# A transformer block on one core: smaller pieces in the gaps between attention scores, rows turned through DRAM

## The chip, the core and the metric

One core of a Trainium2 chip runs the whole program. Its engines work side by side, each through its own list in order: TensorE (PE; its weight loads are shown as PEld), VectorE (DVE), ScalarE (ACT), GpSimd (POOL), and SyncE (SP), which here issues nearly all DMAs. The metric is the device time of one launch in microseconds. Everything is fp32.

## The reference

A pre-norm block: attention with grouped heads and a rotary embedding, then a gated feed-forward part. x is 4 x 512 x 512 (batch, time T, width D), with 32 query heads of 16, 8 key heads, and F = 1376. Cut to what matters:

```python
def attn(x, Wq, Wk, Wv, Wo):
    q, k, v = heads(x @ Wq), heads(x @ Wk), heads(x @ Wv)
    q = q * cos + rotate_half(q) * sin
    k = k * cos + rotate_half(k) * sin
    att = einsum("bhgqd,bhkd->bhgqk", q, k) / sqrt(16)
    att = where(causal, att, -inf)
    ctx = einsum("bhgqk,bhkd->bhgqd", softmax(att), v)
    return merged(ctx) @ Wo

def ffn(x, W_gate, W_up, W_down):
    return (silu(x @ W_gate.T) * (x @ W_up.T)) @ W_down.T

x = x + attn(layernorm(x), Wq, Wk, Wv, Wo)
x = x + ffn(layernorm(x), W_gate, W_up, W_down)
```

## The kernel before

The order of all instructions on every engine is the order in which the Python code issues them; buffers, banks and semaphores follow from it. A matrix product in the code appears in the trace as two passes of TensorE, each with its weight load.

**Groups and visits.** The 4 batches have 8 groups of 4 heads each, 32 in all (`GROUPS`: batch, a pair of two groups `m`, which half `hf`). While group g is exponentiated and averaged, the plain scores of group h = g + 2 are computed to find the greatest of each row, which is then written into rows of `qa` so that the scores of the second computation come out less that value. `slot(b, steps)` does the eight groups of a batch. Each group has four *visits*: `both_scores` (plain scores, L477, in the pair of banks `plain`; the transposed scores less the greatest, L482, in the pair `less`), `exponentials` on ACT (L550), `all_greatest` on DVE (L500, two heads of 512, or of 384 and 128, columns), then `odd_steps(us)`, DVE work from queues, and `gap()`, TensorE work from the slot's list. Then comes `last_visit` (both pairs of banks are used for scores of 256 columns), `turned_round(h)` (a small DVE transpose, L537, and its DMA; `laid_out` reads it back into `qa`), and `averages(g)`: 16 products into the one bank `av` (L576). With `hf == 1` a pair `m` is complete: `later` gets the reads of `av` into `cx` and `us` (L590, L594), a shuffle (L598), four reciprocals (L602), each pair of them with a POOL product into `cx` (L605). `averages` begins with `while unread: do(later)`, since `av` must be read before it is written again; until then `later` is taken from its front.

**The slot's list.** `gap()` takes from the list as much as 1/32 of its total cost says (`fill`; costs are in microseconds). In the first slot it is what is left of batch 1's projections, then those of batches 2 and 3, each behind four `turned` steps; all three batches are attended in later slots. In slots two to four it is the output projection of the batch before (`attended`, L376), its feed-forward part (`hidden`, L420) and the down projection (`down`, L445). `projections` makes keys, queries in four parts, and values of a batch; `portions` cuts a product into steps. A product's bank is one of three (`bank()`, pool `ps_mm`). What follows a product (`finish`: for keys and queries `rotated`, two DVE and two POOL or DVE instructions, L266 to L269) runs at once where `thin[0]` is false; in the opening and the first slot it is put into `full`, with a cost of 1.42.

**The queues of DVE work.** `odd_steps` takes, until its time is down to 0.4, from `full`, from `aside` (statistics of a tile of rows, then its normalisation and, with it, its transpose), from `later`. At the end of `slot` and where a step is due, the queue is emptied by force: `turned`'s `tail(i)` takes from `aside` until tile i is there.

**Turning rows.** Products need the rows' transpose (`xnT`). Batches 0 and 1 are transposed by TensorE against an identity (`transposed`, L221, copy by ACT or DVE, L226 and L224). For the others, and for the rows of every `attended`, `flipped` does it: a DVE transpose of 32 x 32 blocks (L231, two buffers), four DMAs to DRAM (L235), and, for the tile before (at the last tile for both), a read of 256 KB into `xnT` (L237). SP issues these in order, between the weights (L159) and the rows of the greatest (L538, L547).

**The opening.** Rows of batch 0 are normalised, transposed and projected (keys, first query, values), then two masked queries are made on POOL (`masked`, L465), then the plain scores and minima of groups 0 and 1 run with the other queries of batch 0, the transposes of batch 1 and its keys and first query between them. POOL's `rstd` power (L185) is part of the statistics.

Of the kernel before, what the change touches and what calls it, by code (L numbers as in the profile page):

```python
# [15 lines left out]
ALU = mybir.AluOpType  # L16
# [3 lines left out]
NH, NKV, DH = 32, 8, 16  # L20
FF = 1376
P = 128
NT = T // P
NK = D // P
# [50 lines left out]
def preln_block_kernel(  # L75
# [13 lines left out]
    nc = tc.nc  # L89
# [72 lines left out]
    full = deque()  # L162
    thin = [True]

    def bank():
        while len(full) > 1:
            full.popleft()[1]()
        return ps_mm.tile([P, T], F32, tag="mm", name="mm")


# [27 lines left out]
    def do(queue, n=1):  # L198
        for _ in range(min(n, len(queue))):
            queue.popleft()[1]()  # L200

    def odd_steps(us, banks=True):

        for n in range(len(soon)):
            left, step = soon.popleft()
            if left > 0:
                soon.append((left - 1, step))
            else:
                aside.appendleft(step)
        while us > 0.4:  # L210
            others = (unread and later) or aside or later
            queue = (full or others) if banks else (others or full)
            if not queue:
                return
            us -= queue[0][0]
            do(queue)

    def transposed(xn, i, xnT):
        pt = bank()
# [5 lines left out]
        else:  # L225
            nc.scalar.copy(xnT[:, :, ts(i, P)], src)  # L226

    def flipped(xn, i, n, dst):

        t = work.tile([P, D], F32, tag="g", name="xt", bufs=2)  # L230
        nc.vector.transpose(t, xn)  # L231
        turned = flip[n].rearrange("(c d) (i r s) -> i r d c s", d=32, r=4, s=32)
        for r in range(4):
            rows = t[32 * r : 32 * r + 32, :]
            nc.sync.dma_start(out=turned[i, r], in_=rows.rearrange("d (c s) -> d c s", s=32))  # L235
        for a in [i - 1, i] if i == NT - 1 else [i - 1] if i > 0 else []:
            nc.sync.dma_start(out=dst[:, :, ts(a, P)], in_=flip[n].rearrange("(k p) t -> p k t", p=P)[:, :, ts(a, P)])  # L237

    def portions(products, finish, n=2, us=0.0):

        made = {}

        def part(a):
            if a == 0:
                made["ps"] = bank()
            for step in products[len(products) * a // n : len(products) * (a + 1) // n]:
                step(made["ps"])
            if a == n - 1:
                if thin[0]:
                    full.append((us, lambda: finish(made["ps"])))  # L250
                else:
                    finish(made["ps"])

        return [lambda a=a: part(a) for a in range(n)]

    def projected(w, m, xnT, finish):
        def product(ps, k):
            nc.tensor.matmul(ps, lhsT=w[:, k, ts(m, P)], rhs=xnT[:, k, :], start=k == 0, stop=k == NK - 1)  # L258

        steps = [lambda ps, k=k: product(ps, k) for k in range(NK)]  # L260
        return [(0.86, step) for step in portions(steps, finish, 4, 1.42)]

    def rotated(ps, dst, engine=nc.gpsimd):

        rot = work.tile([P, T], F32, tag="rot", name="rot", bufs=4)
        nc.vector.stream_shuffle(rot, ps, ROTATE)  # L266
        engine.tensor_tensor(rot, rot, sin, ALU.mult)
        nc.vector.tensor_tensor(dst, ps, cos, ALU.mult)
        engine.tensor_tensor(dst, dst, rot, ALU.add)  # L269

    def both_steps(measure, norm, tiles=range(NT), cost=1.2):

        for i in tiles:
            yield 1.05, lambda i=i: measure(i)
            if i > 0:
                yield cost, lambda i=i: norm(i - 1)
            if i == NT - 1:
                yield cost, lambda i=i: norm(i)

    def projections(b, n, early=False):  # L280

        home, xa, found, xn = homes[n], {}, {}, {}
        xnT = xnT_of[b]

        def load(i):
# [9 lines left out]
        def norm(i):  # L295
            xn[i] = work.tile([P, D], F32, tag="xa", name="xa", bufs=4) if early else xa[i]
            normalised(xn[i], found[i])
            if b > 1:
                flipped(xn[i], i, b % 2, xnT)

        def keys():
            def finish(ps):
                kr = work.tile([P, T], F32, tag="rot", name="kr", bufs=4)
                rotated(ps, kr, nc.vector if early else nc.gpsimd)

                def spread():
                    ks = work.tile([P, T], F32, tag="rot", name="ks", bufs=4)
                    nc.vector.stream_shuffle(ks, kr, SWAP)
                    for t, hf, src in ((0, 0, kr), (1, 1, kr), (0, 1, ks), (1, 0, ks)):
                        nc.gpsimd.tensor_scalar(  # L310
                            home[:, 4 + 2 * t + hf, :], src, halves[hf], (one16, one0)[hf], ALU.mult, ALU.add
                        )

                if early:
                    spread()
                else:
                    soon.append((1, (0.75, spread)))

            return projected(wk_sb, 0, xnT, finish)

        def vals():
            def product(ps, i, k):
                nc.tensor.matmul(
                    ps[:, ts(i, P)],
                    lhsT=xnT[:, k, ts(i, P)],
                    rhs=wv_sb[:, k, :],
                    start=k == 0,
                    stop=k == NK - 1,
                )

            def finish(ps):
                nc.scalar.copy(
                    values(n)[:, :, :, DH : 2 * DH].rearrange("p i g d -> p (i g) d"),
                    ps.rearrange("p (a d) -> p a d", d=DH),
                )

            steps = [lambda ps, i=i, k=k: product(ps, i, k) for i in range(NT) for k in range(NK)]
            return [(0.9, step) for step in portions(steps, finish, 4)]

        def queries(m):  # L340
            engine = nc.vector if early and m == 0 else nc.gpsimd
# [2 lines left out]
        def begin():  # L344
            for i in range(NT):
                load(i)
            aside.extend(both_steps(measure, norm, cost=1.2 if b > 1 else 0.6))

        def tail(i):
            while i not in xn:  # L350
                do(aside)
            if b < 2:
                transposed(xn[i], i, xnT)

        turned = [(0.45 if b < 2 else 0.0, lambda i=i: tail(i)) for i in range(NT)]
        rest = [*keys(), *queries(0), *vals()]
        for m in range(1, 4):
            rest += queries(m)
        return (0.0, begin), turned, rest

    def attended(b):

        found, xn = {}, {}

        def measure(i):
            found[i] = statistics(xr[b, i])
# [1 line left out]
        def norm(i):  # L368
            xn[i] = work.tile([P, D], F32, tag="xa", name="xn", bufs=4)
            normalised(xn[i], found[i])  # L370
            flipped(xn[i], i, b % 2, xnTs[0])

        def outp(i):
            def product(ps, m):
# [1 line left out]
                nc.tensor.matmul(ps, lhsT=cx[m][:, ts(i, P)], rhs=wo_sb[:, m, :], start=m == 0, stop=m == 3)  # L376

            def finish(ps):
                nc.vector.tensor_tensor(xr[b, i], ps, xr[b, i], ALU.add)
                aside.extend(both_steps(measure, norm, [i]))  # L380

            return [(1.72, step) for step in portions([lambda ps, m=m: product(ps, m) for m in range(4)], finish)]

        def tail():
            while NT - 1 not in xn:
                do(aside)

        def begin():
            if (b, 0) not in xr:
# [1 line left out]
                    load_xr(b, i)  # L391

        first = [(0.0, begin), *(step for i in range(NT) for step in outp(i))]
        return first, [(0.0, tail)]

    wgu = {}

# [11 lines left out]
    def hidden(b, n):  # L409
# [3 lines left out]
        def half(f, a):  # L413
# [8 lines left out]
                )  # L422

            def finish(ps):
                if a == 0:
                    gs[f] = work.tile([P, T], F32, tag="g", name="g", bufs=2)

# [191 lines left out]

    for i in range(NT):  # L620
        load_xr(0, i)
    load_w(wk_sb, wk)
    nc.sync.dma_start(out=rope_sb, in_=rope)
    load_columns(wq_sb, wq, 0, P)
# [8 lines left out]
    load_w(wv_sb, wv)  # L633
    load_columns(wq_sb, wq, P, D)
    load_w(wo_sb, wo)
    for t in low:
        nc.gpsimd.memset(t, 0.0)
    nc.gpsimd.memset(values(0), 1.0)
    thin[0] = False
    for cost, step in turned:  # L640
        step()
    for cost, step in start[:2]:
        step()
    do(aside, len(aside))
    for cost, step in start[2:8]:
        step()
    masked(0)
    masked(1)
    for n in range(1, 4):
        nc.gpsimd.memset(values(n), 1.0)  # L650
    for cost, step in start[8:12]:
        step()


# [15 lines left out]
        return done  # L670

    thin[0] = True
    opening = deque([*start[12:], *turned1, *rest1[:8]])
    each = sum(cost for cost, _ in opening) / 6
    done = 0.0
    for h in range(2):
# [17 lines left out]
    def slot(b, steps):  # L694
# [12 lines left out]
        for g in groups:  # L707
# [6 lines left out]
            for n, visit in enumerate(visits):  # L714
# [13 lines left out]
                all_greatest(h, visit)  # L728
                if n == 2:
                    do(later_act)  # L730
                odd_steps((1.9, 1.9, 1.7, 1.7)[n], n < 3)
                gap()
            last_visit(h, g)
            turned_round(h)
            averages(g)
            odd_steps(1.4)
        thin[0] = False
        do(full, len(full))
        for cost, step in steps:
            step()  # L740

# [16 lines left out]
    def restored():  # L758
        nc.scalar.dma_start(out=homes[1], in_=spill)

    slot(0, [begin2, *rest1[8:], *turned2, begin3, *rest2, *turned3, *rest3[:-16]])

    before, behind = attended(0)
    tiles = list(down(0, 0))
    cut = len(tiles) // 2
    layer = hidden(0, 0)
# [1 line left out]
        1,  # L768
        [
            before[0],  # L770
            *rest3[-16:-8],
            *before[1:],
            after(lambda: load_f(0)),
            *rest3[-8:-1],
            *behind,
            rest3[-1],
            after(lambda: load_f(1)),
# [49 lines left out]
```

## Time and profile before

| what | us |
|---|---|
| median of 3 runs (lowest, highest) | 941.24 (940.16, 943.06) |
| the profiled run's own time | 940.9 |
| its span, first to last instruction | 939.2 |
| PE busy, DVE busy | 894.3, 521.9 |
| ACT busy, POOL busy | 216.4, 217.4 |
| mean granted TensorE clock | 0.995 |

Busy time of TensorE counts each pass until its modelled end, so it is no measure of how densely passes follow each other; the starts are. These are three of the costliest groups of the page, with columns: line, engine, operation, out<-in, shapes and count, then busy us and mean ns of one, then the engine's idle time before them and what ended it:

```profile
L500 DVE CUSTOM_DVE_ANT_0 junk<-sc,mask 128x128 f32<-128x128 f32 (+3 forms) x512 | 250.3, 489 | 163.6 <-PE sc L482 81.2
...
L258 PE MATMUL mm<-xnT,shared 128*128 128x512 f32 x120 | 60.9, 635 | 0.8 <-issue 0.8
...
L602 DVE RECIPROCAL inv<-inv 128x128 f32<-128x128 f32 x64 | 58.0, 932 | 0.5
```

The name behind an arrow is the instruction whose end released the one that waited. In the timeline a row is the start, the length (of several merged instructions together), the engine and line, and in brackets the idle time before it. DMAs are shown by their issue on SP (SPq); when they land is told by the semaphore that they raise.

### The profile page before, as it was taken

What the parts mean: (1) busy time and instruction counts of PE and PEld (TensorE: products, weight loads), DVE (VectorE), ACT (ScalarE), POOL (GpSimd) and SP (SyncE); (2) the same over time, 40 slices, a digit from 0 to 9 for tenths busy, and PEclk for the clock granted to TensorE, in tenths of its full rate; (3) what the DMA queues carried; (4) which work ended last, traced back from release to release, by engine and by line L of the source; (5) the groups of instructions that cost most, each with busy time, mean ns of one, the idle gap of its engine ahead of it and who ended that gap; (6) DMA issues with size and microseconds to landing.
All of it is one profiled execution on the core that took longest, in us unless ns stands there. A gap on an engine that the chain in (4) does not pass through costs nothing.

```text
span 939.2 us, 12679 instructions
## 1 busy us (share of the span) xinstructions
PE 894.3 (95%) x4576; PEld 392.5 (42%) x4576; DVE 521.9 (56%) x1530; ACT 216.4 (23%) x279; POOL 217.4 (23%) x324
## 2 busy tenths in 40 slices
PE   6888889899799999999999999999999999999998
PEld 3443343344344444444444444444444443444443
DVE  7668997778455555475647463686564504322200
ACT  1013333322123232212232322222322320001000
POOL 3554455362321212121112111221111211000000
PEclk9999999999899999999999999999999999999999
DMA  6014140002441520044211110124121101432100
GB/s 223 2 47 91 53 87 3 2 2 48 119 163 50 164 63 24 29 176 97 74 47 47 41 46 13 58 46 103 47 57 47 43 22 68 101 101 75 32 12 34
DMA packets 127871, 60.01 MB, mean 64 GB/s; under 512 B 64608, under 2 KB 119904, under 8 KB 127552
## 3 DMA queue, kind: packets, MB, share of 16 engines
q1 hardware_dynamic: 127520, 53.43, 21.9%
q10 hardware_dynamic: 288, 5.77, 1.6%
q8 instruction: 36, 0.59, 0.3%
q14 instruction: 27, 0.22, 0.1%
HBM read 45.29 MB, written 13.89 MB: 63 GB/s over the span
## 4 chain that ended last, share of the span: by engine, by line
PE 76%; DVE 13%; POOL 4%; issue 3%; DMA 2%; ACT 2%; SPq 0%; POOLq 0%; DVEq 0%
PE mm L420 34%; PE mm L445 16%; PE sc L477 12%; DVE junk L500 6%; PE mm L376 5%; PE sc L482 4%; PE mm L258 3%; POOL qa L465 2%; ACT e L550 2%; POOL e L554 1%; DVE st L182 1%; DVE inv L602 1%; DVE xa L190 1%; DVE xt L231 1%; PE av L576 1%
## 5 line engine op out<-in xcount | busy, mean ns | idle before, releaser
L500 DVE CUSTOM_DVE_ANT_0 junk<-sc,mask 128x128 f32<-128x128 f32 (+3 forms) x512 | 250.3, 489 | 163.6 <-PE sc L482 81.2
L420 PE MATMUL mm<-xnT,shared 128*128 128x512 f32 (+1 forms) x704 | 320.0, 604 | 5.4 <-DMA xnT<-flip 5.4
L550 ACT ACTIVATE e<-sc 128x1024 f32<-128x1024 f32 (+1 forms) x192 | 165.4, 881 | 451.2 <-PE sc L482 357.3
L420 PEld LDWEIGHTS mm<-xnT,shared 128*128 128x128 f32 (+1 forms) x704 | 128.0, 188 | 175.0 <-issue 168.8
L477 PE MATMUL sc<-home,qa 32*128 32x512 f32 (+3 forms) x1024 | 162.3, 459 | 17.8 <-DVE low L500 15.5
L554 POOL TENSOR_SCALAR_AFFINE_SELECT e<-e 128x512 f32<-128x512 f32 (+1 forms) x160 | 85.5, 544 | 392.5 <-ACT e L550 375.6
L482 PE MATMUL sc<-qa,home 32*128 32x512 f32 (+3 forms) x1024 | 163.6, 467 | 1.8 <-DVE low L500 1.7
L445 PE MATMUL mm<-wd_sb,home 128*128 128x512 f32 (+1 forms) x352 | 157.5, 598 | 0.0
L477 PEld LDWEIGHTS sc<-home,qa 32*128 32x128 f32 x1024 | 75.0, 186 | 118.8 <-DVE low L500 35.5
L445 PEld LDWEIGHTS mm<-wd_sb,home 128*128 128x128 f32 (+1 forms) x352 | 65.1, 190 | 83.5 <-issue 82.3
L429 DVE SCALAR_TENSOR_TENSOR g<-g,mm 128x512 f32<-128x512 f32 (+1 forms) x44 | 30.0, 683 | 98.0 <-ACT g L428 98.0
L482 PEld LDWEIGHTS sc<-qa,home 32*128 32x128 f32 x1024 | 71.3, 183 | 31.5 <-issue 14.8
L576 PE MATMUL av<-e,home 128*32 128x512 f32 (+3 forms) x1024 | 77.6, 437 | 1.6 <-POOL e L554 1.6
L428 ACT ACTIVATE g<-mm 128x512 f32<-128x512 f32 (+1 forms) x44 | 26.3, 598 | 181.2 <-PE mm L420 181.2
L258 PE MATMUL mm<-xnT,shared 128*128 128x512 f32 x120 | 60.9, 635 | 0.8 <-issue 0.8
L376 PE MATMUL mm<-wo_sb,cx 128*128 128x512 f32 x128 | 58.7, 603 | 2.4 <-POOL cx L605 2.4
L431 DVE TENSOR_TENSOR home<-mm,g 128x512 f32<-128x512 f32 (+1 forms) x44 | 30.1, 683 | 51.9 <-PE mm L420 51.5
L602 DVE RECIPROCAL inv<-inv 128x128 f32<-128x128 f32 x64 | 58.0, 932 | 0.5
L449 DVE SCALAR_TENSOR_TENSOR xr<-mm,xr 128x512 f32<-128x512 f32 x16 | 10.9, 682 | 76.2 <-PE mm L445 76.2
L576 PEld LDWEIGHTS av<-e,home 128*32 128x32 f32 x1024 | 29.7, 109 | 44.7 <-issue 39.7
L500 DVE DVE_READ_ACCUMULATOR2_ANT low<- 128x1 f32 x512 | 42.2, 82 | 0.0
L605 POOL TENSOR_TENSOR cx<-cx,inv 128x256 f32<-128x256 f32 x32 | 23.2, 725 | 77.3 <-DVE inv L602 77.1
(66 smaller groups left out, 411.7 us busy)
## 6 DMA issues: line engine op xcount, KB each, us to landing
shared<-in_wg SPq DMA_DIRECT2D x40, 256.0 KB
shared<-in_wu SPq DMA_DIRECT2D x40, 256.0 KB
flip<-xt SPq DMA_DIRECT2D x96, 64.0 KB
xnT<-flip SPq DMA_DIRECT2D x24, 256.0 KB
xr<-in_x SPq DMA_DIRECT2D x16, 256.0 KB
out<-xr SPq DMA_DIRECT2D x16, 256.0 KB
xa<-in_x SPq DMA_DIRECT2D x12, 256.0 KB
spill<-wd_sb ACTq DMA_DIRECT2D x1, 2816.0 KB
```

The costliest lines, as they stand in the source:

```text
L258: nc.tensor.matmul(ps, lhsT=w[:, k, ts(m, P)], rhs=xnT[:, k, :], start=k == 0, stop=k == NK - 1)
L376: nc.tensor.matmul(ps, lhsT=cx[m][:, ts(i, P)], rhs=wo_sb[:, m, :], start=m == 0, stop=m == 3)
L420: nc.tensor.matmul(ps[:m, :], lhsT=wgu[c][:, a, k, :m], rhs=xnTs[0][:, k, :], start=k == 0, stop=k == NK - 1)
L431: nc.vector.tensor_tensor(homes[n][:m, f, :], ps[:m, :], gs[f][:m, :], ALU.mult)
L445: nc.tensor.matmul(py[i], lhsT=homes[n][:m, f, ts(i, P)], rhs=wd_sb[:m, f, :], start=f == 0, stop=f == NF - 1)
L477: nc.tensor.matmul(dst, lhsT=qa[g][rows_of(r), ts(i, P)], rhs=k, start=True, stop=True)
L482: nc.tensor.matmul(dst, lhsT=k, rhs=qa[g][rows_of(r), P * j :], start=True, stop=True)
L500: nc.vector.tensor_tensor_reduce(out=junk[:, :n], in0=src, in1=mask[:, T - n :], scale=-1.0, scalar=BIG, op0=ALU.add, op1=ALU.min, accum_o ...
L550: nc.scalar.activation(dst, src, AF.Exp, scale=1.0 / math.sqrt(DH))
L554: nc.gpsimd.affine_select(out=e[:, heads, c : c + P], in_=e[:, heads, c : c + P], compare_op=ALU.is_ge, fill=0.0, base=0, pattern=[[0, hea ...
L576: nc.tensor.matmul(av[32 * r : 32 * r + 32, P * j :], lhsT=v[:, j, 4 * (m // 2) + r, DH * (1 - hf) : DH * (3 - hf)], rhs=e[:, r, c : c + n ...
L602: nc.vector.reciprocal(r[:, ts(n, P)], r[:, ts(n, P)])
```

## The change

- `odd_steps` runs while any queue holds something and stops ahead of a piece that would take the time left below -0.15. In the first slot the times are 1.3, 1.3, 0.95 and 0.95 (before: 1.9, 1.9, 1.7, 1.7, for all slots), in the others 2.3. It stays 1.4 at a group's end.
- `full` holds, for each finished product, a list of pieces with costs of their own: a rotation's two halves (0.73 and 0.69) are taken one by one. A tile's normalisation (0.6) and its transpose (0.75) are two pieces (`norm`, `flip`).
- `projected` computes a product by halves of its columns, in 8 portions of 0.43 (before: 4 of 0.86); the values, too, have 8 portions.
- Rows of batch 1 are turned by `flipped`, not by TensorE. The opening's order is adapted: the keys' portions, six pieces of `aside`, the first query and the values, the rest of `aside`, the masked queries. Two sets of POOL memsets stand earlier.
- `attended(0, by_pe=(2, 3))`: of the first output, tiles 2 and 3 are turned by TensorE in `tail`; tiles 0 and 1 go through DRAM, both reads issued with tile 1.

```diff
+    def emptied(n):
+        for _ in range(n):
+            for _, step in full.popleft():
+                step()
...
-        while us > 0.4:
+        while full or aside or later:
             others = (unread and later) or aside or later
-            queue = (full or others) if banks else (others or full)
-            if not queue:
+            bank = full and full[0]
+            queue = (bank or others) if banks else (others or bank)
+            us -= queue[0][0]
+            if us < -0.15:
                 return
-            us -= queue[0][0]
             do(queue)
+            if full and not full[0]:
+                full.popleft()
...
-        for a in [i - 1, i] if i == NT - 1 else [i - 1] if i > 0 else []:
+        for a in [i - 1, i] if i == last else [i - 1] if i > 0 else []:
...
-                if thin[0]:
-                    full.append((us, lambda: finish(made["ps"])))
-                else:
-                    finish(made["ps"])
+                full.append(deque(finish(made["ps"])))
+                if not thin[0]:
+                    emptied(len(full))
...
-        def product(ps, k):
-            nc.tensor.matmul(ps, lhsT=w[:, k, ts(m, P)], rhs=xnT[:, k, :], start=k == 0, stop=k == NK - 1)
+        def product(ps, k, at):
+            nc.tensor.matmul(
+                ps[:, at], lhsT=w[:, k, ts(m, P)], rhs=xnT[:, k, at], start=k == 0, stop=k == NK - 1
+            )
-        steps = [lambda ps, k=k: product(ps, k) for k in range(NK)]
-        return [(0.86, step) for step in portions(steps, finish, 4, 1.42)]
+        steps = [lambda ps, k=k, h=h: product(ps, k, ts(h, 2 * P)) for h in range(2) for k in range(NK)]
+        return [(0.43, step) for step in portions(steps, finish, 8)]
...
+        return [(0.73, sines), (0.69, cosines)]
...
         for i in tiles:
             yield 1.05, lambda i=i: measure(i)
-            if i > 0:
-                yield cost, lambda i=i: norm(i - 1)
-            if i == NT - 1:
-                yield cost, lambda i=i: norm(i)
+            for a in [i - 1, i] if i == NT - 1 else [i - 1] if i > 0 else []:
+                yield 0.6, lambda a=a: norm(a)
+                yield 0.75, lambda a=a: flip(a)
...
-            if b > 1:
+        def flip(i):
+            if not early:
                 flipped(xn[i], i, b % 2, xnT)
+            ready.append(i)
...
         def tail(i):
-            while i not in xn:
+            while i not in ready:
                 do(aside)
-            if b < 2:
+            if early:
                 transposed(xn[i], i, xnT)
...
+        def flip(i):
+            if i not in by_pe:
+                flipped(xn[i], i, b % 2, xnTs[0], last=NT - 1 - len(by_pe))
+            ready.append(i)
...
         def tail():
-            while NT - 1 not in xn:
+            while NT - 1 not in ready:
                 do(aside)
+            for i in by_pe:
+                transposed(xn[i], i, xnTs[0])
...
-    for cost, step in start[:2]:
+    for cost, step in start[:4]:
+        step()
+    do(aside, 6)
+    for cost, step in start[4:16]:
         step()
     do(aside, len(aside))
-    for cost, step in start[2:8]:
-        step()
     masked(0)
     masked(1)
...
-                odd_steps((1.9, 1.9, 1.7, 1.7)[n], n < 3)
+                odd_steps((1.3, 1.3, 0.95, 0.95)[n] if thin[0] else 2.3, n < 3)
                 gap()
...
-    before, behind = attended(0)
+    before, behind = attended(0, by_pe=(2, 3))
```

In the changed kernel the averages are at L604, the second read of `av` at L622, the projections at L264, the transposes of rows at L238.

## The prediction

> **What bounds the kernel now.** I read the page first: its span, the busy slices, the granted clock and the chain's shares.
>
> ```profile
> span 939.2 us, 12679 instructions
> ...
> PE   6888889899799999999999999999999999999998
> DVE  7668997778455555475647463686564504322200
> ...
> PEclk9999999999899999999999999999999999999999
> ...
> PE 76%; DVE 13%; POOL 4%; issue 3%; DMA 2%; ACT 2%; SPq 0%; POOLq 0%; DVEq 0%
> ```
>
> A slice is 23.5 us. From the twelfth on TensorE is full; what is not TensorE in the chain lies in the first 250 us. So second the stretches, cut at the ends of single groups (columns: stretch and length, then busy time of PE, PEld, DVE, ACT, POOL with counts, granted clock, DMA share, GB/s):
>
> ```profile
> 110.84:128.13 17.29, 14.19 (x110) 5.88 (x108) 16.67 (x48) 6.34 (x8) 9.62 (x13) 1.00 0.32 57
> 128.13:144.88 16.75, 14.99 (x136) 8.50 (x132) 15.61 (x50) 5.66 (x7) 10.35 (x15) 1.00 0.33 73
> 144.88:160.22 15.34, 14.23 (x112) 5.95 (x108) 10.10 (x39) 6.33 (x8) 6.55 (x10) 1.00 0.02 3
> 160.22:178.46 18.24, 14.77 (x112) 5.99 (x108) 16.30 (x52) 5.18 (x6) 9.77 (x13) 1.00 0.02 4
> 178.46:193.76 15.30, 14.12 (x110) 5.88 (x108) 8.73 (x33) 6.34 (x8) 5.83 (x9) 1.00 0.00 1
> ...
> 219.50:251.66 32.16, 26.60 (x136) 11.14 (x132) 18.02 (x56) 6.94 (x9) 10.07 (x13) 0.89 0.50 112
> 251.66:276.04 24.38, 24.33 (x136) 10.51 (x132) 16.20 (x47) 6.38 (x8) 4.79 (x9) 1.00 0.47 163
> ```
>
> The first five are groups 3 to 7 of the eight of the first slot, which take 133.1 us in all (60.67 to 193.76). Groups 5 and 7, with little on DVE, take 15.3; the others up to 18.2. Group 9 takes 32.2 where group 10 takes 24.4, and its clock fell. Third, what a visit and a group's end look like (group 4), and the wait in group 9 (start, length, engine, line, operation):
>
> ```profile
> 138.13 0.72 DVE L598 STREAM_SHUFFLE inv<-us 128x512 f32<-128x512 f32 x1
> 138.26 0.59 PE L477 MATMUL sc<-home,qa 32*128 32x384 f32 x2 [0.83 <-DVE low L500]
> ...
> 141.58 0.71 PE L482 MATMUL sc<-qa,home 32*128 32x256 f32 x8 [0.26 <-DVE low L500]
> 142.12 0.61 PE L477 MATMUL sc<-home,qa 32*128 32x256 f32 x8
> 142.66 2.39 PE L576 MATMUL av<-e,home 128*32 128x512 f32 x32
> ...
> 143.44 0.42 DVE L500 CUSTOM_DVE_ANT_0 junk<-sc,mask 128x256 f32<-128x256 f32 x1 [0.24 <-ACT e L550]
> ...
> 145.41 0.21 DVE L537 STREAM_TRANSPOSE turned<-low 128x32 f32<-128x32 f32 x1
> ```
>
> ```profile
> 234.60 2.38 SPq L235 DMA_DIRECT2D flip<-xt  x4
> ...
> 237.02 2.89 SPq L237 DMA_DIRECT2D xnT<-flip  x2
> ...
> 242.61 5.83 PE L420 MATMUL mm<-xnT,shared 128*128 128x512 f32 x8 [5.39 <-DMA xnT<-flip]
> ```
>
> The plain scores have one pair of banks, so scores, DVE's minima (L500) and the next scores are a loop. In the timeline scores of visits 0 and 2 start 2.66 and 3.05 us before the next ones (60.67 to 63.33; 235.02, its minima over at 237.95, plus 0.1). The minima start 1.18 after the scores and take 1.36 or 1.75. So 1.3 us of other DVE work fits a visit without cost, and what goes over it lengthens the loop. The averages (L576) start right behind the last visit's scores.
>
> **The change, part by part**, against the profiled run's own 940.9 us (span 939.2; the runs' median is 941.24, 0.3 above).
>
> *Halved projections.* 80 products become 160, that is 160 more passes. Passes of 512 columns start 429 ns apart, of 128 columns 112, which is 4.7 over a quarter of 429: 160 x 4.7 ns is 0.8 us. It lies in stretches that wait for DVE: 0; without that cover 0.8.
>
> *The opening* (27.39 to 60.67 before). Removed: 16 transposes on TensorE with their ACT copies; around them (43.4 to 50.4) little else ran and the clock fell for 3.4 us. Added: four DVE transposes of 0.71, 16 writes and 4 reads on SP, behind the weight loads. In the built order DVE has, after the first query's rotation (over at 26.11), transpose 0.71, statistics 1.02 (0.69+0.18+0.15), normalise 0.55, transpose, normalise, transpose. POOL has the power of that statistics (0.75) ahead of the first masked query (0.69), so the first scores start at 29.5 (26.1+0.7+1.1+0.8+0.7), 2.1 late. The last transpose waits for its buffer: the second one's writes are issued from 26.9, 4 x 0.53 (SP's spacing), and land 2.0 after the last issue (flips' median from the semaphore updates), at 30.5; DVE is free at 31.3, not 28.57. From there its blocks (four heads' minima: 3.0, 3.9, 2.0; rotations 1.42, now only behind the blocks): 34.3, 38.3, 40.3, with turn and rotation 42.0, wait for scores to 42.95, then 45.95, 47.4, 51.25, 52.65, 54.6. The first slot starts near 54.8 instead of 60.67: **-5.9** (ends -3.5, if TensorE's 3 us of idling at 26 to 29 halves its clock, and -6.5).
>
> *Budgets in the first slot.* Before, extras per visit go to 2.35; the excess over 1.3 (group 3: 0.49+0.49+0.12+0.28 = 1.4; 15.3+1.4 = 16.7, measured 17.3) explains the long groups. In the new order no visit holds over 1.42 except the forced ones below: 8 x 15.3, plus 0.1 in four groups and 0.7 at the last end (2.1 where 1.4 was) is 123.5. Against 133.1: **-9.6** (ends -5 and -11).
>
> *Where the queue goes.* Nothing was removed from it, so pieces come late and are forced at their due point. Two such points move onto TensorE's path.
>
> (a) Rows of batch 2 (group 2, visit 2) and batch 3 (group 6, visit 2). Before, tiles 2 and 3 are transposed in group 1, visit 0, and group 3, visit 3, ahead of their first product in groups 2 and 6. Now tile 2's transpose, tile 3's normalise and transpose are forced in the very gap in which the keys' first half column is queued, and that product's listed wait is the read of tile 1, which SP issues behind tile 2's four writes. From the scores' start: 1.18+1.75 minima, 0.72 transpose = 3.65; 4 x 0.53 issue; read, issue to landing, 3.0 (2.7 to 3.3; above, the second of two issued near 239.5 is used at 242.6): 8.9; product 0.43; next scores 9.35 instead of 3.05: **+6.3**. In group 6 a reciprocal (0.93) stands ahead: **+7.2**. Queued behind the product are all scores, so ACT and DVE wait too.
>
> (b) Averages of groups 4 and 6. The accumulator must have been read (L594, now L622) before. Before, these reads were in visit 0 or 1. Now reciprocals of the pair before stand ahead of them in `later`, and they are forced after the last visit's minima: the averages' listed wait is L622. From the last visit's start (141.58): turn over 4.0 later (145.6), reciprocal 0.93, two reads 0.72 and 0.74, handover 0.1: 6.5, instead of 1.08. Less 0.6 (bank wait and DVE overhang that this end then lacks): **+4.8 twice, 9.6** (ends 3 and 5.4 each).
>
> (c) The clock. After 5.4 us of idling in group 9 passes came 853 ns apart for 4 us, at the cost of 0.55+4x0.42 = 2.2 us in a stretch bound by TensorE; the stretch's granted clock is 0.89. The four new waits idle TensorE for about 6.9, 7.8, 5.4 and 5.4 us. Here DVE's loop hides part: 1.7 each, **+6.8** (ends 0 and 2.5 each, 10).
>
> The Trainium skill ("TensorE: Matmul & The Clock Gate", on the HAM clock gate) speaks against this change: an idle window of about 3.4 us halves the clock, a busy one restores it. The rows agree, the windows being 3.413 us (48.98 to 52.40) and two of them (240.13 to 246.96). By the page's rule alone each wait would be followed by one or two half-speed windows, an estimate of 1.7 to 3.4 us each, which would make this term 6.8 to 13.6 and the sum 951.0 to 957.8 us.
>
> *Start of the second slot* (group 8). Before, one reciprocal and a POOL product (0.73) separate visit 2's minima from what the first output product needs, a wait of 1.11; now a shuffle (0.73) and a second reciprocal (0.93) come first: **+1.7** (ends 0 and 3).
>
> *First output, two tiles by TensorE* (group 9). The 5.39 wait and the 2.2 behind it go (group 9 is 7.8 over group 10). Tiles 0 and 1 are flipped some 13 us ahead of use. Added: 8 transposes at 0.107, 0.86, and a DVE copy (0.68) behind visit 3's minima: ready 3.75 after the scores where TensorE gets there at 2.8, 0.9. **-6.0** (ends -3 and -7).
>
> Later slots: extras change places in groups that already run at TensorE's pace (24.38): 0; at worst a visit's overhang, 1.
>
> Sum: -5.9 -9.6 +13.5 +9.6 +6.8 +1.7 -6.0 = +10.1, so 951.0; rounded **951 us**.
>
> **Rivals.** (1) *The waits find cover, faster.* Without (a) to (c) the sum is -19.8. Were DVE ahead at the forced points, so that the reads of tile 1 and of the accumulator cost 2 us each and no clock fell, it would be 940.9-19.8+8 = 929. It decides once the forced points cost under 17 in all (29.9 in my sum). For it: DVE is only 57 to 66% busy in groups 5 and 7. Against: DVE's order is fixed, and minima that need the scores just made stand ahead of the forced pieces. (2) *No difference.* No clock falls and the two accumulator waits cost 3 each: 951.0-6.8-3.6 = 940.6. For it: averages could start before all of TensorE's idling counts as a window. Against: group 9. (3) *Budgets bring little, clock costs more.* If the loop and not the excess made the long groups (group 6 also holds a 1.8 us POOL wait), -9.6 becomes -3 and each wait is followed by 2.9: 951.0+6.6+4.8 = 962. For it: group 3 is 0.6 longer than its excess. Against: groups 2 and 4 are within 0.5 of theirs.
>
> **How the numbers follow.** Forecast 0.73, (1) 0.06, (2) 0.08, (3) 0.13. The forecast's own range is 945 to 957: the ends of single terms reach farther, but they are seven and not all on one side. Taking in part of (3) and the edge of (2): 944.5 to 958. What a measurement can tell is 0.3%, 2.8 us: slower is the forecast, (3) and a little of (2), 0.87; same 0.07; faster 0.06.
>
> **What would show it.** Right: waits of the averages for the DVE read of the accumulator, twice, some 5 us; waits of the projection for the DMA of the transposed rows, twice, 6 to 7; none in group 9; half clock behind several of them; groups 0, 1, 3 and 5 near 15.3; first group near 55 us. Wrong: if those four waits are below 2 us, or the groups without forced work stay near 17.

## The result, and the profile after

| | kernel before | changed kernel |
|---|---|---|
| median, us (lowest, highest) | 941.68 (940.16, 943.06) | 950.62 (949.22, 950.80) |
| profiled run's own time, us | 940.9 | 949.2 |
| its span, us | 939.2 | 947.5 |

The ratio is 1.0092, with a 95% interval of 1.0073 to 1.0111: slower, by 8.9 us, where 951 was forecast. First the page of the changed kernel, span, busy slices (now 23.7 us each), granted clock and the chain's shares:

```profile
span 947.5 us, 13021 instructions
...
PE   6898879498999999999999999999999999999998
DVE  7788686568764646377646464576564513421200
...
PEclk9999889699999999999999999999999999999999
...
PE 81%; DVE 10%; POOL 3%; issue 2%; ACT 2%; DMA 2%; SPq 0%; POOLq 0%; DVEq 0%
```

The dip of the clock in the eleventh slice (group 9) is gone. A deeper hole stands in the eighth: TensorE 4 tenths busy at a granted clock of 6 tenths. From the eleventh slice on TensorE is as full as before. Busy shares hardly tell it: DVE is busy 523.4 us where it was 521.9. The stretches do, cut at the ends of groups as before (groups 2 to 6, then group 9; same columns):

```profile
83.10:107.05 23.95, 16.81 (x124) 9.51 (x120) 14.45 (x48) 5.19 (x6) 7.67 (x11) 0.86 0.42 100
107.05:122.61 15.56, 14.33 (x124) 8.23 (x120) 13.15 (x48) 6.34 (x8) 8.25 (x12) 1.00 0.13 20
122.61:144.73 22.12, 16.00 (x140) 9.51 (x136) 17.24 (x53) 5.66 (x7) 11.92 (x16) 0.85 0.02 4
144.73:159.61 14.88, 13.96 (x124) 7.95 (x120) 10.19 (x37) 6.34 (x8) 5.29 (x8) 1.00 0.18 36
159.61:191.93 32.32, 19.25 (x124) 10.32 (x120) 18.89 (x56) 5.18 (x6) 11.30 (x14) 0.74 0.21 43
...
234.34:258.80 24.46, 23.77 (x156) 13.54 (x152) 16.72 (x54) 6.85 (x9) 9.99 (x13) 1.00 0.43 105
```

Groups 3 and 5 are down from 17.29 and 15.34 us to 15.56 and 14.88: a visit's DVE work now fits. Groups 2, 4 and 6 are up from 16.62, 16.75 and 18.24, and only in these three is the clock below 1. Group 2 of the kernel before, the first stretch of the first slot that grew, was:

```profile
94.22:110.84 16.62, 14.77 (x112) 5.99 (x108) 15.87 (x53) 5.18 (x6) 7.61 (x12) 1.00 0.20 66
```

The table of TensorE's waits (us in total, times, longest) names the reason:

```profile
PE mm L264 <- DMA xnT<-flip: 14.6, 2, 7.7
PE av L604 <- DVE us L622: 10.2, 2, 5.1
...
PE mm L396 <- POOL cx L633: 4.1, 2, 2.6
PE sc L505 <- POOL qa L493: 2.7, 1, 2.7
```

The first two rows are four waits: 24.8 us, one in group 2, one in group 4, two in group 6. The timeline shows how each comes about. First the rows of batch 2 in group 2, visit 2 (start, length, engine, line, operation, idle time before and its releaser):

```profile
89.11 0.59 PE L505 MATMUL sc<-home,qa 32*128 32x384 f32 x2
...
92.04 0.71 DVE L238 STREAM_TRANSPOSE xt<-xa 128x512 f32<-128x512 f32 x1
...
92.78 1.95 SPq L242 DMA_DIRECT2D flip<-xt  x4
94.77 0.51 SPq L244 DMA_DIRECT2D xnT<-flip  x1
95.38 2.12 SPq L242 DMA_DIRECT2D flip<-xt  x4
...
98.21 1.19 PE L264 MATMUL mm<-xnT,shared 128*128 128x256 f32 x2 [6.89 <-DMA xnT<-flip]
```

Read it backwards: the keys' product (98.21) waits for the read issued at 94.77; SP issues that behind four writes; these wait for a transpose that DVE starts at 92.04, behind the minima of the scores of 89.11. From the scores to the product it is 9.1 us (8.9 in the forecast), and all later scores are queued behind it. Its two passes take 1.19 us, at half clock (0.65 at full clock, in experiment 4). Second, the accumulator at the end of group 4, beside the view shown of before:

```profile
134.76 0.71 PE L510 MATMUL sc<-qa,home 32*128 32x256 f32 x8 [0.43 <-DVE low L528]
...
138.60 0.21 DVE L565 STREAM_TRANSPOSE turned<-low 128x32 f32<-128x32 f32 x1
138.73 0.91 DVE L630 RECIPROCAL inv<-inv 128x128 f32<-128x128 f32 x1
...
139.56 0.65 DVE L618 SCALAR_TENSOR_TENSOR cx<-av,rope_sb,cx 128x512 f32<-128x512 f32 x1
...
140.13 0.74 DVE L622 SCALAR_TENSOR_TENSOR us<-av,rope_sb,us 128x512 f32<-128x512 f32 x1
...
141.02 3.90 PE L604 MATMUL av<-e,home 128*32 128x512 f32 x32 [5.11 <-DVE us L622]
```

The averages start 6.26 us behind the last visit's scores, where before it was 1.08, since a reciprocal of the pair before and the two reads stand between the turn and them. They then take 3.90 us for work that took 2.39.

### The profile page after: what moved, and what is told of

It is laid out like the page before. It is cut to its first block, busy times and chain, and to the rows that moved or that the text cites. A ratio compares the mean times of both kernels' runs of the same rounds, so it can differ in the third digit from the quotient of the medians.

```text
span 947.5 us, 13021 instructions
## 1 busy us (share of the span) xinstructions
PE 896.1 (95%) x4728; PEld 424.5 (45%) x4728; DVE 523.4 (55%) x1533; ACT 214.8 (23%) x276; POOL 218.0 (23%) x324
## 4 chain that ended last, share of the span: by engine, by line
PE 81%; DVE 10%; POOL 3%; issue 2%; ACT 2%; DMA 2%; SPq 0%; POOLq 0%; DVEq 0%
PE mm L445 33%; PE mm L473 16%; PE sc L505 14%; PE mm L396 6%; DVE junk L528 5%; PE sc L510 5%; PE mm L264 4%; PE av L604 2%; ACT e L578 2%; POOL qa L493 2%; POOL e L582 1%; PE mm L336 1%; DMA xnT<-flip 1%; DVE inv L630 1%; DVE st L186 1%
## 5 line engine op out<-in xcount | busy, mean ns | idle before, releaser
L510 PE MATMUL sc<-qa,home 32*128 32x512 f32 (+3 forms) x1024 | 165.6, 471 | 2.6 <-DVE low L528 2.6
L604 PE MATMUL av<-e,home 128*32 128x512 f32 (+3 forms) x1024 | 80.3, 453 | 10.2 <-DVE us L622 10.2
L457 DVE SCALAR_TENSOR_TENSOR g<-g,mm 128x512 f32<-128x512 f32 (+1 forms) x44 | 29.9, 680 | 88.0 <-ACT g L456 88.0
L264 PE MATMUL mm<-xnT,shared 128*128 128x256 f32 x240 | 64.7, 414 | 14.6 <-DMA xnT<-flip 14.6
L264 PEld LDWEIGHTS mm<-xnT,shared 128*128 128x128 f32 x240 | 46.2, 203 | 31.8 <-issue 24.2
L604 PEld LDWEIGHTS av<-e,home 128*32 128x32 f32 x1024 | 30.8, 112 | 54.8 <-issue 47.6
```

Source lines behind the costliest of these rows:

```text
L264: nc.tensor.matmul(ps[:, at], lhsT=w[:, k, ts(m, P)], rhs=xnT[:, k, at], start=k == 0, stop=k == NK - 1)
L510: nc.tensor.matmul(dst, lhsT=k, rhs=qa[g][rows_of(r), P * j :], start=True, stop=True)
L604: nc.tensor.matmul(av[32 * r : 32 * r + 32, P * j :], lhsT=v[:, j, 4 * (m // 2) + r, DH * (1 - hf) : DH * (3 - hf)], rhs=e[:, r, c : c + n ...
```

## The experiments

Experiments 1 to 8 are small edits of the changed kernel, so its 950.62 us is the figure to compare with; 9 to 12 start from the fifth. Each was timed beside the kernel before, whose median was 941.0 to 942.6 in these sessions; ratios are to it.

**1 to 3: the due points.** The first edit forces the outstanding reads of the accumulator in visit 3, ahead of the last visit; the second moves the `turned` steps 8 portions earlier in the list; the third has both.

```diff
                 odd_steps((1.3, 1.3, 0.95, 0.95)[n] if thin[0] else 2.3, n < 3)
+                while n == 3 and thin[0] and unread:
+                    do(later)
```
```diff
-    slot(0, [begin2, *rest1[16:], *turned2, begin3, *rest2, *turned3, *rest3[:-32]])
+    slot(0, [begin2, *rest1[16:-8], *turned2, *rest1[-8:], begin3, *rest2[:-8], *turned3, *rest2[-8:], *rest3[:-32]])
```

> The changed kernel, with one due point moved: in the first slot the two reads of the accumulator that are still outstanding are forced in visit 3's gap, and no longer behind the last visit's minima. All other work is the same. My theory (the forced reads stand on TensorE's path only because of where they are due): the two waits of 5.29 us in groups 4 and 6 vanish, DVE's overhang in visit 3 costs 1.7 us each (2.96 us of pieces where 1.3 fit), and the half-clock windows behind both waits go (0.3 to 1.7 each): 950.6 - 10.6 + 3.4 - 2 = 941.4 us (939 to 943.5). Rival, DVE's load sets the first slot, wherever its pieces stand: 948 to 951.

> The changed kernel, with the other due point moved: the steps that demand the turned rows of batches 2 and 3 stand 8 portions (2.7 gaps) earlier in the first slot's list, so the same transposes are forced one or two gaps before the keys' first product. My theory (TensorE waits for the chain transpose, four writes, read): the waits of 7.06 and 7.86 us in groups 2 and 6 vanish, DVE's overhang costs 1.5 us each, and half clock behind the waits goes (about 3 in all): 950.6 - 14.9 + 3.1 - 3 = 935.8 us (933 to 939). Rival, DVE's load: 948 to 951. Rival, the reads themselves are slow (SP's queue or the transfers): waits of 3 us and more stay, 942 to 947.

> Both due points moved (as in the two runs before). My theory: the gains add, 950.6 - 9.2 - 14.8 = 926.6 us (923 to 931), below the kernel before by about 15. Rival, the backlog only shows again at the next place (the first output of the second slot): 935 to 945, with a wait of over 8 us at the start of group 8.

Measured: 941.39 us (ratio to before 1.0001, 0.9992 to 1.0010), 940.78 (0.9995, 0.9983 to 1.0007) and 929.98 (0.9883, 0.9870 to 0.9896). Nothing was taken from DVE in any of them (busy 523.0 to 524.2 us, 523.4 in the changed kernel). Moving when the pieces are due gains 9.2, 9.8 and, together, 20.6 us, so DVE's load is not the cause, and the backlog does not come out elsewhere: group 8's wait for POOL's product stayed at 2.6. The waits of the first edit:

```profile
PE mm L264 <- DMA xnT<-flip: 14.5, 2, 7.7
...
PE av L604 <- DVE us L622: 2.8, 2, 1.9
```

The rows' waits are untouched, the accumulator's fall from 10.2 to 2.8. The second edit missed its interval by 2 us: its waits for DMA are gone (0.2 us is left), but the forced transposes hold up the next scores by 2.9 us in group 2 and 1.8 in group 6 (I had 1.5 each), a half-clock window follows each of the two (from 94.23 and from 165.91 us; I had none there), and its profile has one more in the opening, worth 1.4 (see 9):

```profile
PE av L604 <- DVE us L622: 10.2, 2, 5.1
PE sc L505 <- DVE low L528: 8.8, 12, 2.9
```

**4: the clock alone.** Eight idle products keep TensorE busy while it waits for the rows; the product that follows overwrites their bank (`busy` is true for the keys of batches 2 and 3).

```diff
             if a == 0:
                 made["ps"] = bank()
+                for k in range(8 if busy else 0):
+                    nc.tensor.matmul(made["ps"], lhsT=wo_sb[:, k % 4, :P], rhs=wo_sb[:, k % 4, :], start=True, stop=True)
```

> The changed kernel, with 8 idle products of 128 x 512 (16 passes, about 6.9 us) into the keys' own bank ahead of the keys' first product of batches 2 and 3, whose start=True product overwrites them: TensorE is busy while it waits for the turned rows, nothing else changes. It measures the clock alone. My forecast's term (1.7 us behind each wait): 947.2 us (945.5 to 948.5), and no half-clock window behind the two waits for DMA. Rival, half clock lies in DVE's loop and costs nothing: 950.6. Rival, the 2.9 each of the forecast's third rival: 944.8.

947.56 us (1.0072, 1.0054 to 1.0091), 3.1 less; the six runs spread from 945.73 to 951.63, so the groups below are the firmer evidence. The wait is as long as before, but filled (first row: the 16 idle passes; second row: the keys' product):

```profile
92.28 7.03 PE L254 MATMUL mm<-wo_sb 128*128 128x512 f32 x16
99.15 0.65 PE L266 MATMUL mm<-xnT,shared 128*128 128x256 f32 x2
```

The keys' two passes now take 0.65 us, not 1.19. Groups 2 and 6 are 0.97 and 2.53 us shorter: 1.75 on average, as the forecast had it, though the two are unlike: group 2 gave 1.1 us back, as its averages took 3.50 us instead of 2.39 and waited for POOL's `e`. What the clock still costs in group 6, and all that it costs in group 4, is behind the waits for the accumulator.

**5 and 6: budgets that leave no backlog.**

```diff
-                odd_steps((1.3, 1.3, 0.95, 0.95)[n] if thin[0] else 2.3, n < 3)
+                odd_steps((1.9 if g < 2 else 1.6) if thin[0] else 2.3, n < 3)
```

The sixth has `(1.9, 1.9, 1.7, 1.7)[n]` there, the budgets of before.

> The changed kernel with one line changed: the first slot's budgets are 1.9 in groups 0 and 1 and 1.6 in all others, instead of 1.3, 1.3, 0.95, 0.95. In the order of instructions nothing is forced any more before the second slot: the last transpose of batch 2 stands in group 1, of batch 3 in group 5, and the reads of the accumulator two visits ahead of the averages. My theory (only the forced points cost): 950.6 - 25.5 for the four waits - 5 for the clock behind them + 1.6 of overhang (pieces of up to 1.73 us where 1.3 fit) - 1 at the start of group 8 (one reciprocal and a shuffle fewer) = 920.7 us (917 to 924). Rival, the backlog only moves: 928 or more, with a new wait of over 2 us in the first slot. Rival, budgets above 1.3 cost what they cost before (groups of 16.5 to 17.3 us): 930.

> The changed kernel with the first slot's budgets of before (1.9, 1.9, 1.7, 1.7); the split pieces and the new rule for stopping stay. Nothing is forced here either; the overhang over 1.3 us per visit sums to 5.4 us by the order of the pieces, against 2.5 in the run with 1.9 and 1.6. My theory: 920.7 + 2.9 = 923.6 us (920 to 927). Rival, the smaller budgets themselves were the gain (the forecast's 9.6 us): 930 to 933.

919.82 us (0.9773, 0.9758 to 0.9788) and 921.95 (0.9793, 0.9779 to 0.9806). With *more* DVE work allowed per visit the kernel is 31 us faster than the changed one (29 in the sixth). Groups 2 to 6 of the fifth:

```profile
85.83:101.55 15.72, 14.34 (x124) 8.23 (x120) 13.81 (x47) 5.19 (x6) 7.16 (x11) 1.00 0.37 107
101.55:117.20 15.65, 14.37 (x124) 8.26 (x120) 14.18 (x50) 6.34 (x8) 9.75 (x13) 1.00 0.12 19
117.20:132.75 15.55, 14.41 (x140) 9.08 (x136) 13.37 (x45) 5.66 (x7) 9.58 (x14) 1.00 0.11 17
132.75:148.14 15.39, 14.29 (x124) 8.23 (x120) 14.40 (x48) 6.34 (x8) 6.40 (x10) 1.00 0.47 93
148.14:163.72 15.58, 14.34 (x124) 8.23 (x120) 13.79 (x45) 5.18 (x6) 7.33 (x11) 1.00 0.07 18
```

All within 0.35 us of each other, at full clock, with DVE between 13.4 and 14.4 us in each: the work is spread, where the tight budgets left 10.2 in group 5 and 18.9 in group 6. None of the four waits is in either trace.

**7 and 8: two parts undone.** Batch 1 transposed by TensorE again (the new order of the opening kept); all of the first output through DRAM again.

```diff
-            if not early:
+            if b > 1:
                 flipped(xn[i], i, b % 2, xnT)
...
-            if early:
+            if b < 2:
                 transposed(xn[i], i, xnT)
...
-        turned = [(0.0, lambda i=i: tail(i)) for i in range(NT)]
+        turned = [(0.45 if b < 2 else 0.0, lambda i=i: tail(i)) for i in range(NT)]
```
```diff
-    before, behind = attended(0, by_pe=(2, 3))
+    before, behind = attended(0, by_pe=())
```

> The changed kernel with one part undone: batch 1's rows are transposed by TensorE again, with ACT's copies; the order of the opening stays the new one. Forecast's term, 5.9 us: 956.5. The trace of the changed kernel puts opening and group 0 together at 10.2 us less, of which 1.7 was to come from budgets; if all the rest is this part: 959. Rival, most of the opening's gain is the new order around it (first scores at 26.2 us instead of 27.4 although the forecast had 29.5): 951 to 954.

> The changed kernel with one part undone: all four tiles of the first output go through DRAM again. Forecast's term, 6.0 us: 956.6. By group 9's own difference between the two profiles, 7.7: 958.3, with a wait of the hidden layer's first product for the DMA of over 5 us in group 9 and half clock behind it. Rival, the wait was gone anyway by the other budget in this slot (2.3): 950.6.

952.58 us (1.0116, 1.0100 to 1.0133) and 953.29 (1.0133, 1.0114 to 1.0152): 2.0 and 2.7 us by the medians, 2.6 and 3.5 by the spans of the profiles, where the forecast gave these parts 5.9 and 6.0. In the seventh the first slot still starts at 56.7 us, not 60.7 as before (52.8 in the changed kernel), so half of that gain is the opening's new order; of the other half 1.4 is a half-clock window in this profile. In the eighth the wait of group 9 is back, but shorter than the 5.39 of before:

```profile
PE mm L445 <- DMA xnT<-flip: 3.7, 1, 3.7
```

So the rest of the change brings the rows 1.7 us sooner; the second slot's larger budget is the likely part of it, which was not tried by itself.

**9 to 12: on top of the even budgets.** Three idle products behind the values, where TensorE waits for the first masked query; 1.6 in group 0 too; projections by whole columns; and, on the ninth, POOL's memsets back at their old place.

```diff
+    for k in range(3):
+        nc.tensor.matmul(plain[:, 0, :], lhsT=wk_sb[:, k, :], rhs=xnTs[0][:, k, :], start=True, stop=True)
```
```diff
-                odd_steps((1.9 if g < 2 else 1.6) if thin[0] else 2.3, n < 3)
+                odd_steps((1.9 if g == 1 else 1.6) if thin[0] else 2.3, n < 3)
```
```diff
-        steps = [lambda ps, k=k, h=h: product(ps, k, ts(h, 2 * P)) for h in range(2) for k in range(NK)]
+        steps = [lambda ps, k=k: product(ps, k, slice(0, T)) for k in range(NK)]
```
```diff
-    nc.gpsimd.memset(values(0), 1.0)
-    for t in low:
-        nc.gpsimd.memset(t, 0.0)
     load_w(wk_sb, wk)
...
     load_w(wo_sb, wo)
+    for t in low:
+        nc.gpsimd.memset(t, 0.0)
+    nc.gpsimd.memset(values(0), 1.0)
```

> The run with the even budgets, and three products of 128 x 512 (6 passes, 2.6 us) into the scores' bank behind the values, where TensorE waits for the first masked query; the scores overwrite them. Its profile had a half-clock window at 26.1 to 29.5 us, right behind that wait of 3.8, and took 28.0 us from the first scores to the first slot where profiles without such a window took 26.6. If the idle wait is what lowers the clock: 919.8 - 1.4 = 918.4 us (917.5 to 919.5) and no window at 26. Rival, nothing changes or the products delay the scores: 919.8 to 921.5.

> The run with the even budgets, but 1.6 in group 0 too (1.9 in group 1 alone). Group 0 took 16.3 us there against 14.7 with small budgets, so it gives back up to 1.6; batch 2's last transpose then comes in group 2, visit 1, one visit ahead of the keys' first product. If the transposed rows are in time: 918.5 us (917.5 to 919.5). Rival, the second half column waits for tiles 2 and 3: 919.5 to 922, with a wait for DMA of 1 to 3 us in group 2.

> The run with the even budgets, and projections over whole columns again (4 products of 512 columns; every second portion is empty). The forecast costed halving at 0 where TensorE waits for DVE, 0.8 without cover: 919 to 920 us. Rival, halves even out the gaps: without them a gap holds 0.86 or 1.72 us of TensorE work instead of 1.29, the larger ones lengthen visits, up to 0.4 in 16 of them: 922 to 926.

> The run with the busy opening, with the memsets of the values' tile and of the minima's tiles back where they stood before (behind batch 0's statistics on POOL). In the profile of the kernel before, DVE's last normalisation of batch 0 took 1.75 us, not 0.55, while such a memset of 1.37 ran on POOL (9.8 to 11.6 us); in the changed kernel, with the memsets earlier, 0.55. If the two engines hold each other up there: that normalisation takes 1.6 to 1.8 us again, the first scores come about 1.2 us later, 918.1 + 1.2 = 919.3 us (918.6 to 920). Rival, the long normalisation was chance or is hidden: 0.55 us, and 917.7 to 918.5.

The ninth took 918.08 us (0.9743, 0.9729 to 0.9757), 1.7 less than the fifth, with no half-clock window before the end: the fastest version found, 2.6% under the kernel before. The eleventh took 920.71 (0.9779, 0.9762 to 0.9795), not to be told from the fifth by the interval, and between what I expected and the rival; its groups 1 to 7 sum to 110.0 us against 108.7, so in the trace halves gain some 1.2 us, which the forecast's 0 left out.

The tenth failed both its expectations: 927.39 us (0.9840, 0.9824 to 0.9855). A budget smaller by 0.3 in one group delays everything behind it, and in group 6 the second read of the accumulator is forced again, behind the last visit's turn:

```profile
167.08 0.21 DVE L565 STREAM_TRANSPOSE turned<-low 128x32 f32<-128x32 f32 x1
167.22 0.71 DVE L622 SCALAR_TENSOR_TENSOR us<-av,rope_sb,us 128x512 f32<-128x512 f32 x1
...
168.07 3.76 PE L604 MATMUL av<-e,home 128*32 128x512 f32 x32 [3.68 <-DVE us L622]
```

I had looked at the rows of batch 2 alone. Group 6 takes 20.3 us instead of 15.6, and two half-clock windows in the opening come on top. Groups 2 and 4 are 1.2 and 1.7 us longer too; there the averages wait for POOL's `e`, 2.1 us in all.

The twelfth took 919.00 us (0.9765, 0.9750 to 0.9780), 0.9 more than the ninth, and its first scores come 0.9 later (27.29 against 26.39 us). DVE's normalisation is as long again as the memsets beside it:

```profile
9.44 0.23 POOL L665 MEMSET low<- 128x32 f32 x3
9.52 1.75 DVE L194 TENSOR_SCALAR xa<-xr,mv,rstd 128x512 f32<-128x512 f32 x1 [0.44 <-POOL rstd L189]
9.61 1.37 POOL L666 MEMSET home<- 128x1536 f32 x1
```

## Why the prediction was right, point by point

| step | forecast, us | measured, us |
|---|---|---|
| opening, to the start of the first slot | -5.9 | -7.9 (60.7 to 52.8) |
| first slot without waits and clock | -9.6 | -11.2 |
| (a) waits for batch 2's and 3's rows | +6.3, +7.2 | +7.1, +7.9 |
| (b) waits of the averages, twice | +4.8 each | +5.3 each |
| (c) clock behind the four waits | +6.8 | +6.7 |
| start of the second slot | +1.7 | +1.7 |
| first output | -6.0 | -6.0 |
| later slots | 0 | -0.5 |
| sum | +10.1 | +8.4 (the spans: +8.35) |

Measured terms come from the two profiles. The first slot went from 133.1 to 154.1 us; the waits are TensorE's lost time between passes there; the clock is 3.5 from experiment 4 and 3.2 from the two lengthened blocks of averages (3.83 and 4.29 against 2.44, from their first pass to the next scores); what then remains is 121.9. Group 8 went from 25.7 to 27.4. Group 9 lost 7.7, of which 1.7 only moved to group 11 with two steps of the list (22.66 to 24.38).

The rows of (a) and (b) are not quite alike in the two columns: measured is all time that TensorE lost there, forecast what is added to a visit or to a group's end. Counted as the forecast counts, (a) is +6.5 and +7.3: from scores to next scores it is 10.22 us (89.11 to 99.33) and 11.04 (165.61 to 176.65), less the 3.05 of before, less 0.69 that the product loses to half clock (1.12 us to the next scores where the forecast had 0.43). And (b) is +4.6 each (6.26 and 6.33 instead of 1.08, less the forecast's 0.6). The row above them is then -8.7, not -11.2, and the sum stays. So the waits were forecast within 0.2 us each, and the largest miss is the opening's 2.0.

That 951 came within 0.4 us of the median is partly luck. By the spans the forecast is 1.7 too high (+10.1 against +8.35); the changed kernel's median lies 1.4 above its profiled run, and that made up for most of it. Some of its sums are also 0.1 to 0.2 high by their own terms (first scores 29.3, not 29.5; the chain of (a) 8.8, not 8.9).

*(a), (b): right, and shown to be causal.* Mechanism, places and sizes hold, and experiments 1 to 3 take each away by its due point alone. The first rival, that the waits find cover, needed them under 17 in all; they cost 32 with the clock (30 as the forecast counts, which had 29.9). The second had no clock term; experiment 4 shows 3.1 us of it on the waits for the rows alone.

*The opening: the step that failed.* The end of "the first query's rotation (over at 26.11)" was carried over from the old profile, and the new pieces were put behind it. But it ends at 22.96, so that the first scores come at 26.16 instead of the forecast's 29.5:

```profile
22.26 0.70 DVE L281 TENSOR_TENSOR home<-home,rot 128x512 f32<-128x512 f32 x1
...
24.71 0.71 POOL L189 TENSOR_TENSOR rstd<-rstd,neghalf 128x1 f32<-128x1 f32 x1 [1.19 <-DVE rstd L188]
25.42 1.52 POOL L493 TENSOR_SCALAR qa<-home,rope_sb 128x512 f32<-128x512 f32 x2
...
26.16 1.14 PE L505 MATMUL sc<-home,qa 32*128 32x512 f32 x8 [2.71 <-POOL qa L493]
```

The chain was right (rotation, transpose and statistics, power on POOL, masked query), its origin 3.2 us off. Two things had moved it. The last tile's statistics and two normalisations of batch 1 now stand behind that rotation, one transpose ahead of it (0.69+0.18+0.15, 0.55 twice, less 0.71: 1.4 us). And the memsets, named in the change but not costed, no longer hold up a normalisation of batch 0: 1.2 us in DVE's rows, 0.9 in the time by experiment 12. A wait of DVE for POOL's power (0.44) that fell away is most of the rest. Of the 3.2 us, 1.3 was lost again up to the first slot (26.7 us from the first scores, 25.3 in the forecast).

*Right sums, wrong owners.* The opening's gain was put down to TensorE's transposes; undoing them costs 2.0 us (2.6 by the spans), and the new order has most of the rest. The first output's 6.0 was put down to the two tiles by TensorE; undoing that costs 2.7 (3.5 by the spans); the rest goes with the rows that come earlier. The first slot's 9.6 was put down to the small budgets; with the old ones and the new pieces (experiment 6) the slot takes 127.3 us, 5.7 of the gain, with 1.6 and 1.9 it takes 125.1, 8.0. So the third rival's suspicion was half right: the small budgets bring some 3 us over the old ones (8.7 against 5.7), and that only before the waits that they cause. That the long groups came from excess work fits (groups 3 and 5 fell to 15.56 and 14.88 us), but the excess was not varied by itself.

What stays open: how much of the 5.7 us the split pieces and the rule that stops ahead of a piece bring each; they were not tried apart. Halved products are some 1.2 of it, if what experiment 11 shows for the even budgets holds here.

## What to carry to other kernels

A budget that keeps each gap clean does not remove work, it builds a queue, and a queue with due points pays at the worst place: where the piece is demanded by the engine that sets the time. Before tightening a budget, list what is forced, where, and what is queued behind it; either move the due points ahead of the use by the length of the whole chain, or raise the budget until nothing is forced. When an order changes, rebuild start times from the first moved instruction; a start time taken over from the old profile is no longer a row of the new one.

## What the hardware showed

All half-clock windows inside the programs were one to three times 3.413 us long. In each profile they start whole multiples of 3.413 us apart, on one grid, which lies at another phase in each run, and how long TensorE idled did not settle whether one came. Ahead of the first scores 2.9 us of lost time in the changed kernel brought none; 2.6 us in experiment 7 brought one (26.69 to 30.10 us). In that run 2.24 us of the idle time fell into one window of the grid (23.28 to 26.69); in the other at most 1.5 did, since the boundary at 24.72 cut it in two. The Trainium skill ("TensorE: Matmul & The Clock Gate", Part 1 on the HAM clock gate) calls the window free-running, and these runs agree; it asks for an idle window, and here one that was idle for two thirds was enough. In experiment 2 a wait of 1.76 us did it, about half of a window: TensorE waits from 162.85 to 164.61, inside the window from 162.50 to 165.91, and half clock follows at 165.91. How much of a window must be idle these runs do not settle. In the opening such a window costs 1.4 us: from the first scores to the first slot it is 26.6 to 26.7 us in the profiles without one (the changed kernel, experiments 1, 3, 6, 8, 9 and 12), 28.0 with one (2, 4 and 5) and 29.4 with two (10).

The second: a DVE normalisation (128x512) beside POOL memsets took 1.75 us instead of 0.55, twice (the kernel before, experiment 12), and ended 0.29 us behind the memset. The Trainium skill ("SBUF — State Buffer", "Who interferes with whom") says that the two engines share a pair of ports, that `tensor_scalar` can take it, and that the one which issues later is blocked for the whole instruction of the other. The rows fit in that DVE waits out the memsets. But in experiment 12 its normalisation, which starts at 9.52 beside the short memset, also waits out the long one that starts behind it, at 9.61.
